# Expert tiles laid out in pairs: one weight load and 256-column operations for 14 of 23 tiles

## The chip, the cores and the metric

The kernel runs on one core of one Trainium2 chip. A core has TensorE (PE, and PEld for its weight loads), ScalarE (ACT), VectorE (DVE), GpSimd (POOL) and SyncE (SP), and 16 DMA engines that all queues share. The metric is the device time of one execution in microseconds, lower is better; the time given is the median of the runs.

## What is computed

The input is 16 sequences of 256 tokens with 128 features, 4096 tokens in all, in float32. Two layers follow each other. Each is a sandwich: half a mixture of experts, attention, half a mixture of experts, each on the layer-normalized input and added to it.

```python
x = x + 0.5 * ffn0(layernorm(x))     # 8 routed experts, top 2 by softmax, and a shared one; SwiGLU, 128 wide
x = x + attn0(layernorm(x))          # 16 heads of 8, difference of two softmaxes, a layer norm on the output
x = x + 0.5 * ffn0(layernorm(x))
x = x + 0.5 * ffn1(layernorm(x))     # 8 experts, top 2, shares normalized; a * gelu(g), 256 wide
x = x + attn1(layernorm(x))          # 16 heads of 8, causal, with an output projection
x = x + 0.5 * ffn1(layernorm(x))

# ffn1, for each token t and each of its two experts e:
hidden = xt[t] @ W1[e] + b1[e]
a, g = split(hidden)
out[t] += share[t, e] * ((a * gelu(g)) @ W2[e] + b2[e])
```

The reference computes every expert for every token and weights by zero where an expert isn't chosen. Only the two chosen experts count.

## The kernel before

**Parts and stages.** The 4096 tokens are 8 blocks of 512 (four chunks of 128). A part of an expert layer is two blocks, 1024 tokens and so 2048 pairs of token and expert. The first part of the first expert layer is computed densely, every expert for every token (`dense`), which fills the start. All other parts are sparse (`Sparse`): seven of two blocks in layer 0, seven of two blocks and two of one block in layer 1. The attention of a block runs in between, sequence by sequence (`Attention`).

**A sparse part.** `dispatch` normalizes the blocks, computes the gates, chooses two experts for each token (`choose`), and counts on VectorE how many tokens each expert has. Tiles of 128 slots belong to one expert each. With `nch` chunks there are `2 * nch + E - 1` tiles: 23 for two blocks, 15 for one, enough for any routing with 8 experts. `first` is the number of tiles of the earlier experts, `slot` the place of each token, `idx` its two slots. `scatter` writes the normalized rows to `slots_x` in HBM with indirect DMAs on GpSimd. Then `dispatch` compares the tile's number with each expert's `end` and so finds the expert of each tile; `rows` holds its row in `wcat`, an HBM array with all weights and biases of one expert side by side.

`load_tiles` works in steps of two tiles. For each tile SyncE reads a register from `rows` and issues one DMA of that expert's weights into a buffer of `b_wt` (257 KB in layer 0, 450 KB in layer 1); every second step it loads four tiles of `slots_x` into `xg`. `compute` takes two tiles: two transposes on TensorE, a copy into `xT`, then the first matmuls. For each tile, each half z of the hidden layer and each 128 hidden features k there is one matmul of 128 columns, with its own weights, into the PSUM buffer `hid` (tiles `big`). ScalarE applies bias and activation, in operations of 128 columns because the bias belongs to the tile's expert; layer 0 needs two of them for each (`swiglu`), layer 1 one. VectorE adds the other bias and multiplies into `h`. The second matmuls have `h` as the stationary operand and give tokens on partitions. VectorE adds the output bias tile by tile into `y`, SyncE writes `y` to `slots_y`. When all tiles of a part are stored, `combine` gathers each token's two rows on GpSimd and `add_to_x` adds them with their shares on VectorE.

**What sets the order.** Every engine's order is written out when the kernel is built. Each piece of work is a generator that says with `Ask` which engine it needs, what it reads and which buffers it takes. `Tasks.run` starts, again and again, the piece with the smallest expected start plus `HASTE` times its rank. `Clocks` and `Timed` keep the expected times; `MARGIN` is a slack by engine. The ranks of the parts (`FFN_RANK`) and of the attention of each block (`ATT_RANK`) are lists of numbers. Each engine then executes in the written order, and a later instruction does not pass one that waits.

**Buffers.** Three `big` PSUM buffers of two banks are shared by attention scores and hidden layers; two further banks are cut into halves (`half`). `b_wt` has six buffers and gets three more, and `b_xg` two and three more, from tiles of the dense stage (`rw`, `cwb` in the profile) once that is done. So a group `big<-xT,rw` does the same work as `big<-xT,wt`, and `cwb<-slots_x` is a load of `xg`. Nearly all operations are recorded at line 136, that of the helper that passes them on, so the profile's groups are told apart by their tiles.

A float32 matmul appears in the trace as two passes, each with a weight load.

Of the kernel before, what the change touches and what calls it, by code (L numbers as in the profile page):

```python
# [9 lines left out]
FP = mybir.dt.float32  # L10
BF = mybir.dt.bfloat16
I32 = mybir.dt.int32
# [13 lines left out]
TABLE = 2.0  # L26
LATE = 1.5
LATE_ROWS = 2.0
MARGIN = {"PE": 1.0, "ACT": 1.25, "DVE": 1.5, "POOL": 1.25, "SP": 2.0}
HASTE = 0.0048  # L30

FFN_RANK = [
    [63, 53, 104],
    [190, 217, 235, 249],
    [218, 230, 258, 292],
    [422, 440, 392, 493, 452],
]
ATT_RANK = [
    [75, 122, 109, 110, 131, 132, 238, 239],
    [259, 260, 308, 281, 348, 311, 320, 528],  # L40
]


# [210 lines left out]
def kernel(ctx: ExitStack, tc: tile.TileContext, a: dict, out: bass.AP):  # L254
# [37 lines left out]
    PCH = PB * NCH  # L292
    NTILE = 2 * PCH + E - 1
    NSLOT = NTILE * P
    BIG = 1 << 14
    assert NSLOT < BIG

# [41 lines left out]
    def buffers(n, shape, name, dtype=FP):  # L339
# [26 lines left out]
            for i in range(4)  # L366
# [23 lines left out]
                tile_of(shape, name)  # L390
                for name, shape in (
                    ("cntb", [P, P]), ("pos", [P, PCH * E + E]), ("low", [P, PCH, E]),
                    ("high", [P, PCH, E]), ("slot", [P, PCH, E]), ("over", [P, NTILE, E]),
                    ("little", [P, 128]),
                )
            )
# [156 lines left out]
        (a["L0_ffn_rw1"], a["L0_ffn_rw2"], a["L0_ffn_rb2"]),  # L553
        (a["L1_ffn_W1"], a["L1_ffn_W2"], a["L1_ffn_b2"]),
    ]
    wcat = [dram.tile([E * P, WC[layer]], FP, name=f"wcat{layer}") for layer in range(2)]

    for layer in range(2):
        clocks.expect(wcat[layer], E // 4 + KF[layer] + 2)

    def gather_weights(layer, b1t, *deps):
        w1, w2, b2 = srcs[layer]
        wc, col = wcat[layer], W1C[layer]
        v = wc.rearrange("(e p) f -> e p f", p=P)
        todo = [(v[e : e + 4, :, 0:col], w1[e : e + 4]) for e in range(0, E, 4)]
        for k in range(KF[layer]):
            todo += [(v[:, :, col : col + C], w2[:, k * P : (k + 1) * P, :])]
            col += C
        todo.append((v[:, :, col : col + C], b2.unsqueeze(1).to_broadcast([E, P, C])))
        col += C  # L570
        nk = 2 * KF[layer]
        for o, i in todo:
            yield Ask("SP", after=max(0.0, clocks.bytes_free - 3.0))
            nc.sync.dma_start(out=o, in_=i)
        yield Ask("SP", deps, after=max(0.0, clocks.bytes_free - 3.0))
        nc.sync.dma_start(
            out=wc[:, col : col + nk].rearrange("(e p) k -> p e k", p=P),
            in_=b1t.rearrange("p (e k) -> p e k", k=nk),
        )
# [34 lines left out]
    same = tile_of([P, E], "same")  # L614
    sums_ce = tile_of([P, PCH * E + E], "sums_ce")

    full = tile_of([P, E, PCH], "full")
    bare.gpsimd.iota(
        full, pattern=[[0, E], [P, PCH]], base=0, channel_multiplier=0,
        allow_small_or_imprecise_dtypes=True,  # L620
    )
    number = tile_of([P, NTILE, E], "number")
    bare.gpsimd.iota(
        number, pattern=[[1, NTILE], [0, E]], base=0, channel_multiplier=0,
        allow_small_or_imprecise_dtypes=True,
    )

    own4 = tile_of([P, 4, G], "own4")
    bare.gpsimd.memset(own4, 1.0)
# [325 lines left out]
    idx_of, rows_of, wgt_of = [], [], []  # L955
    for i in range(NFFN):
        idx_of.append(tile_of([P, 2, PCH], f"idx{i}", I32))
        rows_of.append(tile_of([P, NTILE], f"rows{i}", I32))
        wgt_of.append(tile_of([P, 2, PCH], f"wgt{i}"))

    def transfers(todo, when=None, pool=None):
# [16 lines left out]
    class Sparse:  # L978
        def __init__(self, index, layer, which, blocks, slots, rank, last=False):
            self.layer, self.last, self.rank = layer, last, rank  # L980
            self.after = 3 * layer + 2 * which
            self.blocks = blocks
            self.nch = len(blocks) * NCH
            self.ntile = 2 * self.nch + E - 1
            self.sx, self.sy = slots_x[slots], slots_y[slots]
            self.rows = rows_of[index]
            self.idx, self.wgt = (t[index][:, :, : self.nch] for t in (idx_of, wgt_of))
            self.gated = self.out_tiles = self.stored = 0
            self.scattered, self.weighed = [], False
            self.ready = False  # L990
            self.left = [NCH * 2 + (BPB if layer == 0 else 0) for _ in self.blocks]
# [20 lines left out]
        def dispatch(self):  # L1012
# [5 lines left out]
            for i, n in enumerate(self.blocks):  # L1018
# [9 lines left out]
            nch, ntiles = self.nch, self.ntile  # L1028
            cntb, pos, low, high, slot, over, little = tmp
            low, high, slot = (t[:, :nch] for t in (low, high, slot))  # L1030
            over = over[:, :ntiles]
            s3, N = [P, nch, E], nch * E

            tk = taken.rearrange("p c e -> p (c e)")
            cnt, ntile, first, end = (little[:, 16 * i : 16 * i + w] for i, w in enumerate((1, E, E, E)))
            _, (t,) = yield pe(taken, take=[(half, 1)])
            nc.tensor.matmul(t[:N, 0:1], lhsT=tk, rhs=ones[:, 0:1], start=True, stop=True)
            yield vec(t)
# [11 lines left out]
            nc.vector.tensor_tensor(  # L1050
                pv, pos[:, :E].unsqueeze(2).to_broadcast([P, E, nch]), full[:, :, :nch], ALU.is_gt
            )
            nc.vector.tensor_reduce(ntile, pv, AX.X, ALU.add)
            pe2 = over.rearrange("p n e -> p (n e)")[:, : E * E].rearrange("p (e f) -> p e f", e=E)
            nc.vector.tensor_tensor(
                pe2, earlier, ntile.unsqueeze(1).to_broadcast([P, E, E]), ALU.mult
            )
            nc.vector.tensor_reduce(first, pe2, AX.X, ALU.add)
            nc.vector.tensor_tensor(end, first, ntile, ALU.add)
            nc.vector.tensor_scalar(first, first, float(P), None, ALU.mult)  # L1060
            nc.vector.tensor_tensor(
                slot, pos[:, E : N + E].rearrange("p (c e) -> p c e", e=E),
                first.unsqueeze(1).to_broadcast(s3), ALU.add,
            )

            yield vec(slot)
            at = little[:, 64 : 64 + 2 * nch].rearrange("p (j c) -> p j c", j=2)
# [6 lines left out]
            tasks.add(self.rank - 6, self.scatter(xns))  # L1074

            yield vec(end)
            expert = cntb[:, :ntiles]
            nc.vector.tensor_tensor(
                over, number[:, :ntiles], end.unsqueeze(1).to_broadcast([P, ntiles, E]), ALU.is_ge
            )  # L1080
            nc.vector.tensor_reduce(expert, over, AX.X, ALU.add)
            nc.vector.tensor_scalar(self.rows[:, :ntiles], expert, float(E - 1), float(P), ALU.min, ALU.mult)
            self.ready = True

            yield vec(at, low)
# [85 lines left out]

        def load_tiles(self):

            layer, ntiles = self.layer, self.ntile
            for j in range(0, ntiles, 2):
                js = range(j, min(j + 2, ntiles))
                _, wts = yield Ask(
                    "SP", (self.rows, wcat[layer]), take=[(b_wt, len(js))],
                    when=lambda: self.ready and len(self.scattered) == 2 * self.nch,
                )  # L1180
                if j % 4 == 0:
                    n = min(4, ntiles - j)
                    _, at = bare.values_load_multi_w_load_instructions(
                        self.rows[0:1, j : j + n], engines=[ENG.SP], min_val=0, max_val=(E - 1) * P,
                        skip_runtime_bounds_check_because="a minimum of E - 1 and a count, by P",
                    )
                    clocks.free["SP"] += 0.8
                for i, wt in zip(js, wts):
                    row = at[i % 4]
                    clocks.free["SP"] += 0.2  # L1190
                    nc.sync.dma_start(out=wt[:, : WC[layer]], in_=wcat[layer][bass.ds(row, P), :])
                if j % 4 == 0:
                    _, (xg,) = yield Ask("SP", (self.sx,), take=[(b_xg, 1)])
                    ld = nc.sync.dma_start(
                        out=xg[:, :n],
                        in_=self.sx[j * P : (j + n) * P, :].rearrange("(i p) d -> p i d", p=P),
                    )
                    for s in self.scattered:
                        tc.add_manual_dep(ld.ins, s.ins.name, SYNC, reason="every row may be here")
# [2 lines left out]

        def compute(self, j, wts, xg, i0, last):
            layer = self.layer
            K, n = KF[layer], len(wts)
            w2, bias = W1C[layer], W1C[layer] + K * C + C
            act0, lin0 = (0, 1) if layer == 0 else (K, 0)
            _, (t, xT) = yield pe(xg, take=[(half, 1), (b_xT, 1)])
# [4 lines left out]
            yield from move(xT[:, : n * P], t[:, : n * P])  # L1213
            half.put(t)
            _, (hid, h) = yield pe(xT, *wts, take=[(big, 1), (b_h, 1)])
            at = [(i, k, slice((i * K + k) * P, (i * K + k + 1) * P)) for i in range(n) for k in range(K)]
            for z, base in ((0, act0), (1, lin0)):
                for i, k, cs in at:
                    nc.tensor.matmul(
                        hid[:, z, cs], lhsT=wts[i][:, (base + k) * P : (base + k + 1) * P],  # L1220
                        rhs=xT[:, i * P : (i + 1) * P], start=True, stop=True,
                    )
            b_xT.put(xT)
            tiles = [
# [1 line left out]
                    cs, wts[i][:, bias + act0 + k : bias + act0 + k + 1],  # L1226
                    wts[i][:, bias + lin0 + k : bias + lin0 + k + 1],
                )
                for i, k, cs in at
            ]  # L1230
            if layer == 0:
                yield from swiglu(hid, h, tiles)
# [16 lines left out]
                    start=(k == 0), stop=(k == K - 1),  # L1249
                )  # L1250
            b_h.put(h)
            for i in range(n):
                yield vec(t)
                nc.vector.tensor_tensor(
                    y[:, i, :], t[:, i * P : (i + 1) * P], wts[i][:, w2 + K * C : w2 + (K + 1) * C],
                    ALU.add,
                )
            half.put(t)
            b_wt.put(*wts)

            self.out_tiles += n
            late = 3.0 if self.out_tiles < self.ntile else 0.0
# [451 lines left out]
```

## Time and profile before

| | |
|---|---|
| Median of 3 timed runs | 1543.52 us (1541.05 to 1553.22) |
| The profiled execution | 1429.88 us, span 1428.2 us |
| Mean granted TensorE clock in the span | 0.93 |
| Bytes moved by DMA | 232.87 MB, mean 163 GB/s |
| Weight loads of expert tiles | 235 into `wt`, 117 into `rw` |
| Dispatches (indirect DMAs) | 240 scatters, 240 gathers |

The profiled execution is shorter than the timed runs by 113.6 us. All durations of instructions are from it, so sums are to be compared with its own time.

A row of a group gives the line, engine, operation, tiles written and read, shape and count; then the busy time in us and the mean duration of one in ns; then the idle time of the engine just before them and what ended it. The busy time of a group counts overlapping instructions once, so busy time divided by the count is what one costs in a dense run, and the mean is what one takes from its start to its end. A row by stretches gives for each engine the busy time and the number of instructions, then the granted TensorE clock, the mean busy share of the DMA engines and the rate.

### The profile page before, as it was taken

Reading aid. Unit: us, or ns where it says so; the run is one execution under the profiler, and the core shown is the slowest. Engines: PE = TensorE matmul, PEld = TensorE weight load, DVE = VectorE, ACT = ScalarE, POOL = GpSimd, SP = SyncE. Lnnn points to the kernel's source line nnn. Section 1 sums busy time; section 2 is a strip of 40 time slices with the busy share of each in tenths; the row PEclk is TensorE's granted clock in tenths of the full one; section 3 lists DMA queues with packets and bytes.
Section 4 is the critical chain, followed back from the end, with each engine's and each line's share of the span. In section 5 each row is a group of like instructions: output and inputs, shape, how many; then the busy total and the mean of one; then the engine's idle time right before and its main releaser. Section 6 shows DMA issues by size and latency. Waiting matters only on the chain. (4 is left out here: it accounts for less than half of the span.)

```text
span 1428.2 us, 29288 instructions
## 1 busy us (share of the span) xinstructions
PE 1189.7 (83%) x9730; PEld 810.9 (57%) x9730; DVE 932.9 (65%) x3259; ACT 803.2 (56%) x1710; POOL 612.9 (43%) x623
## 2 busy tenths in 40 slices
PE   5848899998989999998888888888679888887773
PEld 3414566555445544566755755676367676657672
DVE  5456876867555667674776778877854763885553
ACT  2212477766767776775666565556437665554331
POOL 2010545431630143616154466453752764665324
PEclk8766999999999999999999999999879999999997
DMA  5075577753125111567656655772168544658893
GB/s 121 20 165 150 184 201 207 196 166 93 53 89 140 40 27 35 177 198 229 194 160 215 203 155 170 231 230 88 45 226 254 170 169 156 206 191 283 271 305 111
DMA packets 207532, 232.87 MB, mean 163 GB/s; under 512 B 32062, under 2 KB 151545, under 8 KB 207371
## 3 DMA queue, kind: packets, MB, share of 16 engines
q1 hardware_dynamic: 192010, 199.42, 46.4%
q0 software_dynamic: 15360, 31.49, 7.0%
q8 instruction: 79, 1.29, 0.4%
q14 instruction: 83, 0.67, 0.2%
HBM read 183.84 MB, written 52.75 MB: 166 GB/s over the span
## 5 line engine op out<-in xcount | busy, mean ns | idle before, releaser
L136 ACT ACTIVATE ex<-big 128x1024 f32<-128x1024 f32 (+1 forms) x384 | 349.1, 957 | 76.8 <-PE big L136 71.4
L1117 POOL DMA_INDIRECT slots_x<-xn,idx x240 | 239.8, 999 | 213.8 <-PE bank L136 62.4
L1276 POOL DMA_INDIRECT g<-slots_y,idx x240 | 238.7, 994 | 196.2 <-PE big L136 75.1
L136 PE MATMUL big<-q,k 32*128 32x512 f32 (+1 forms) x1536 | 235.4, 613 | 5.5 <-DVE h L136 3.3
L136 PE MATMUL big<-xT,wt 128*128 128x128 f32 x1452 | 202.0, 285 | 15.6 <-ACT xT L136 9.9
L136 PEld LDWEIGHTS big<-xT,wt 128*128 128x128 f32 x1452 | 183.8, 199 | 29.1 <-ACT xT L136 16.0
L136 POOL TENSOR_TENSOR rstd<-rstd,mhalf 128x4 f32<-128x4 f32 (+1 forms) x64 | 62.1, 970 | 319.3 <-DVE rstd L136 311.6
L136 PE MATMUL bank<-ex,vaug 128*32 128x256 f32 (+1 forms) x3072 | 177.6, 371 | 11.7 <-DVE ex L136 4.1
L136 ACT ACTIVATE s<-big,wt 128x128 f32<-128x128 f32 x470 | 137.9, 384 | 69.1 <-PE big L136 56.9
L136 DVE SCALAR_TENSOR_TENSOR h<-big,wt,s 128x128 f32<-128x128 f32 x363 | 105.9, 342 | 47.5 <-ACT s L136 46.4
L136 PEld LDWEIGHTS bank<-ex,vaug 128*32 128x32 f32 x3072 | 89.8, 111 | 81.7 <-issue 13.6
L136 PE MATMUL bank<-wt,h 128*128 128x128 f32 x726 | 116.2, 294 | 21.4 <-DVE h L136 7.6
L136 DVE SCALAR_TENSOR_TENSOR x<-g,wgt,x 128x128 f32<-128x128 f32 x240 | 86.7, 364 | 71.8 <-DMA g<-slots_y,idx 70.6
L136 PEld LDWEIGHTS bank<-wt,h 128*128 128x128 f32 x726 | 96.9, 199 | 52.3 <-ACT xT L136 12.2
L136 ACT COPY xT<-bank 128x256 f32<-128x256 f32 x183 | 63.2, 375 | 110.6 <-PE bank L136 82.5
L136 PE MATMUL big<-xT,rw 128*128 128x128 f32 x720 | 107.4, 289 | 5.1 <-ACT xT L136 2.9
L136 PEld LDWEIGHTS big<-q,k 32*128 32x128 f32 x1536 | 74.9, 186 | 64.2 <-issue 39.4
L136 DVE TENSOR_TENSOR y<-bank,wt 128x128 f32<-128x128 f32 x235 | 59.2, 283 | 70.0 <-PE bank L136 34.4
L136 PEld LDWEIGHTS big<-xT,rw 128*128 128x128 f32 x720 | 96.5, 203 | 10.0 <-ACT xT L136 4.2
L136 POOL TENSOR_TENSOR ex<-ex,causal 128x512 f32<-128x512 f32 x52 | 65.5, 1281 | 77.8 <-ACT ex L136 68.2
L136 ACT COPY avs<-bank 128x256 f32<-128x256 f32 x96 | 36.1, 376 | 91.2 <-PE bank L136 68.0
L136 ACT ACTIVATE s<-big,rw 128x128 f32<-128x128 f32 x234 | 70.9, 382 | 17.7 <-PE big L136 16.8
(192 smaller groups left out, 1819.4 us busy)
## 6 DMA issues: line engine op xcount, KB each, us to landing
wt<-wcat SPq DMA_DIRECT2D x128, 450.0 KB
rw<-wcat SPq DMA_DIRECT2D x63, 450.0 KB
wt<-wcat SPq DMA_DIRECT2D x107, 257.0 KB
slots_y<-y SPq DMA_DIRECT2D x168, 128.0 KB
rw<-wcat SPq DMA_DIRECT2D x54, 257.0 KB
cwb<-slots_x SPq DMA_DIRECT2D x45, 256.0 KB
xg<-slots_x SPq DMA_DIRECT2D x31, 256.0 KB
slots_x<-zero SPq DMA_DIRECT2D x12, 384.0 KB
```

The source lines that it names most:

```text
L136: r = f(*args, **kw)
L1117: s = bare.gpsimd.indirect_dma_start(out=self.sx[:, :], out_offset=bass.IndirectOffsetOnAxis(ap=self.idx[:, j, c : c + 1], axis=0), in_=ro ...
L1276: s = bare.gpsimd.indirect_dma_start(out=g[:, :], out_offset=None, in_=self.sy[:, :], in_offset=bass.IndirectOffsetOnAxis(ap=self.idx[:, j ...
```

## The change

The slots of a part are laid out anew. Each expert's tiles are first taken in twos: `own[:, 0]` counts an expert's pairs of tiles, `own[:, 1]` its odd tile (0 or 1). All pairs come first in the slots, then the single tiles. The first `nch - 1` steps of two tiles are always pairs of one expert: 7 for a part of two blocks (14 of 23 tiles), 3 for a part of one block (6 of 15). The remaining 9 tiles are single ones, as before. The counts are such that this holds for any routing; an eighth pair, where there is one, lies in two single tiles.

A unit is a pair or a single tile; a part has 16 of them (12 with one block). `rows` holds one entry for each unit and `load_tiles` issues one weight load for each. In `compute`, a pair has one set of weights. Its first matmuls, its activations, its products and its bias addition are single operations on both tiles, 256 columns wide, where there were two of 128. For that `hid` and `h` are ordered by hidden feature first and tile second. Transposes, second matmuls, copies to `xT` and stores of `y` stay.

In `dispatch`, the counting is done for pairs and singles at once (twice as wide), the slot of a token gets a further term `beyond` where its place lies behind its expert's pairs, and the expert of a unit comes from two comparisons, one for the pairs and one for the singles, the latter counted from the end. `wcat` becomes twice as tall with the weights in the upper half, since the sum of the two comparisons starts at 8.

`HASTE`, two margins and the ranks have other numbers.

```diff
-MARGIN = {"PE": 1.0, "ACT": 1.25, "DVE": 1.5, "POOL": 1.25, "SP": 2.0}
-HASTE = 0.0048
+MARGIN = {"PE": 1.0, "ACT": 1.0, "DVE": 1.5, "POOL": 1.25, "SP": 1.5}
+HASTE = 0.003
 FFN_RANK = [
-    [63, 53, 104],
-    [190, 217, 235, 249],
-    [218, 230, 258, 292],
-    [422, 440, 392, 493, 452],
+    [80, 66, 114],
+    [190, 217, 315, 246],
+    [218, 225, 258, 290],
+    [424, 437, 433, 444, 408],
 ]
 ATT_RANK = [
-    [75, 122, 109, 110, 131, 132, 238, 239],
-    [259, 260, 308, 281, 348, 311, 320, 528],
+    [77, 132, 109, 110, 131, 132, 158, 159],
+    [319, 320, 342, 339, 406, 369, 373, 551],
 ]
...
+            self.npair = self.nch - 1
+            self.nunit = self.npair + E + 1
...
+            nc.vector.tensor_reduce(own[:, 0], pv[:, :, 1::2], AX.X, ALU.add)
             nc.vector.tensor_reduce(ntile, pv, AX.X, ALU.add)
-            pe2 = over.rearrange("p n e -> p (n e)")[:, : E * E].rearrange("p (e f) -> p e f", e=E)
+            nc.vector.scalar_tensor_tensor(own[:, 1], own[:, 0], -2.0, ntile, ALU.mult, ALU.add)
+            s4 = [P, 2, E, E]
...
             nc.vector.tensor_tensor(
-                pe2, earlier, ntile.unsqueeze(1).to_broadcast([P, E, E]), ALU.mult
+                pe2, earlier.unsqueeze(1).to_broadcast(s4), own.unsqueeze(2).to_broadcast(s4), ALU.mult
             )
             nc.vector.tensor_reduce(first, pe2, AX.X, ALU.add)
-            nc.vector.tensor_tensor(end, first, ntile, ALU.add)
-            nc.vector.tensor_scalar(first, first, float(P), None, ALU.mult)
-            nc.vector.tensor_tensor(
-                slot, pos[:, E : N + E].rearrange("p (c e) -> p c e", e=E),
-                first.unsqueeze(1).to_broadcast(s3), ALU.add,
-            )
+            nc.vector.tensor_tensor(end, first, own, ALU.add)
+            nc.vector.tensor_scalar(start, first[:, 0], 2.0 * P, None, ALU.mult)
+            nc.vector.tensor_scalar(inside, own[:, 0], 2.0 * P, None, ALU.mult)
+            nc.vector.scalar_tensor_tensor(beyond, end[:, 0], 2.0, first[:, 1], ALU.mult, ALU.add)
+            nc.vector.tensor_scalar(
+                beyond, beyond, -float(P), float(P * (ntiles - 1)), ALU.mult, ALU.add
+            )
+            place = pos[:, E : N + E].rearrange("p (c e) -> p c e", e=E)
+            yield vec(pos)
+            nc.vector.tensor_tensor(slot, place, start.unsqueeze(1).to_broadcast(s3), ALU.add)
+            nc.vector.tensor_tensor(low, place, inside.unsqueeze(1).to_broadcast(s3), ALU.is_ge)
+            nc.vector.tensor_tensor(low, low, beyond.unsqueeze(1).to_broadcast(s3), ALU.mult)
+            nc.vector.tensor_tensor(slot, slot, low, ALU.add)
...
+            nc.vector.tensor_scalar(start, end[:, 0], 2.0, -2.0 * self.npair, ALU.mult, ALU.add)
             nc.vector.tensor_tensor(
-                over, number[:, :ntiles], end.unsqueeze(1).to_broadcast([P, ntiles, E]), ALU.is_ge
+                over[:, :, 0:E], number[:, -self.nunit :], start.unsqueeze(1).to_broadcast(s3u), ALU.is_ge
+            )
+            nc.vector.tensor_tensor(
+                over[:, :, E:], follow[:, -self.nunit :], end[:, 1].unsqueeze(1).to_broadcast(s3u), ALU.is_ge
             )
...
             for j in range(0, ntiles, 2):
-                js = range(j, min(j + 2, ntiles))
+                nwt = 1 if u < self.npair else min(2, ntiles - j)
                 _, wts = yield Ask(
-                    "SP", (self.rows, wcat[layer]), take=[(b_wt, len(js))],
+                    "SP", (self.rows, wcat[layer]), take=[(b_wt, nwt)],
...
-            K, n = KF[layer], len(wts)
+            K, n = KF[layer], min(2, self.ntile - j)
+            one = len(wts) < n
+            wts = wts * n if one else wts
...
-            at = [(i, k, slice((i * K + k) * P, (i * K + k + 1) * P)) for i in range(n) for k in range(K)]
+            at = [(i, k, slice((k * n + i) * P, (k * n + i + 1) * P)) for i in range(n) for k in range(K)]
+            if one:
+                both = [(0, k, slice(k * n * P, (k + 1) * n * P)) for k in range(K)]
+            else:
+                both = at
             for z, base in ((0, act0), (1, lin0)):
-                for i, k, cs in at:
+                for i, k, cs in both:
                     nc.tensor.matmul(
                         hid[:, z, cs], lhsT=wts[i][:, (base + k) * P : (base + k + 1) * P],
-                        rhs=xT[:, i * P : (i + 1) * P], start=True, stop=True,
+                        rhs=xT[:, : n * P] if one else xT[:, i * P : (i + 1) * P], start=True, stop=True,
                     )
...
-            for i in range(n):
+            tn = t[:, : n * P].rearrange("p (i c) -> p i c", c=C)
+            for i in range(1 if one else n):
+                si = slice(0, n) if one else slice(i, i + 1)
+                b2 = wts[i][:, w2 + K * C : w2 + (K + 1) * C].unsqueeze(1)
                 yield vec(t)
                 nc.vector.tensor_tensor(
-                    y[:, i, :], t[:, i * P : (i + 1) * P], wts[i][:, w2 + K * C : w2 + (K + 1) * C],
-                    ALU.add,
+                    y[:, si, :], tn[:, si, :], b2.to_broadcast([P, si.stop - si.start, C]), ALU.add
                 )
```

## The prediction

> **What bounds the kernel now.** I read the page's head first, then the busy time by stages, then the groups with shapes kept apart, the waits of TensorE, and the transfers of the last stage. The page's chain of waits covers only the last 46 us, so the bound has to be read from the stages.
>
> ```profile
> span 1428.2 us, 29288 instructions
> PE 1189.7 (83%) x9730; PEld 810.9 (57%) x9730; DVE 932.9 (65%) x3259; ACT 803.2 (56%) x1710; POOL 612.9 (43%) x623
> ```
>
> ```profile
> core 0: us, PE busy (x) PEld busy (x) DVE busy (x) ACT busy (x) POOL busy (x), PEclk, DMA share, GB/s
> 0.00:160.00 160.00, 108.05 (x306) 58.11 (x307) 90.30 (x270) 39.21 (x78) 24.32 (x44) 0.77 0.50 127
> 160.00:640.00 480.00, 450.05 (x4034) 259.54 (x4032) 322.52 (x1128) 343.17 (x665) 177.36 (x183) 1.00 0.43 124
> 640.00:1000.00 360.00, 300.85 (x2520) 227.43 (x2523) 263.57 (x931) 214.46 (x479) 182.24 (x181) 0.94 0.61 188
> 1000.00:1080.00 80.00, 59.20 (x496) 42.28 (x489) 52.29 (x193) 35.83 (x78) 51.06 (x49) 0.83 0.42 143
> 1080.00:1280.00 200.00, 174.33 (x1601) 133.88 (x1599) 130.26 (x446) 124.31 (x267) 115.11 (x103) 0.96 0.59 187
> 1280.00:1405.00 125.00, 97.21 (x785) 89.65 (x785) 68.54 (x280) 46.23 (x146) 50.90 (x53) 0.95 0.85 277
> ```
>
> See here: from 160 to 640 us (mostly layer 0) TensorE is busy 450 of 480 us at full clock. It sets the pace, and only shorter TensorE work can help much. From 640 to 1405 us (mostly layer 1's experts) it is busy 631.6 of 765 us: 133 us are idle, the clock is below 1, and no other engine is full. That is a chain of hand-overs between engines, with the DMA engines at 0.85 in the last 125 us.
>
> ```profile
> L136 PE MATMUL big<-xT,wt 128*128 128x128 f32 x1452 | 202.0, 285 | 15.6 <-ACT xT L136 9.9 <-ACT ex L136 4.7 <-ACT s L136 0.4
> L136 ACT ACTIVATE s<-big,wt 128x128 f32<-128x128 f32 x470 | 137.9, 384 | 69.1 <-PE big L136 56.9 <-issue 8.5 <-ACT ex L136 1.0
> L136 DVE SCALAR_TENSOR_TENSOR h<-big,wt,s 128x128 f32<-128x128 f32 x363 | 105.9, 342 | 47.5 <-ACT s L136 46.4 <-PE bank L136 0.8
> L136 DVE TENSOR_TENSOR y<-bank,wt 128x128 f32<-128x128 f32 x235 | 59.2, 283 | 70.0 <-PE bank L136 34.4 <-ACT xT L136 13.4 <-ACT s L136 7.3
> L136 ACT ACTIVATE s<-big,b_0t 128x512 f32<-128x512 f32 x64 | 40.5, 684 | 59.1 <-PE big L136 56.7 <-issue 1.5 <-DVE h L136 0.7
> L136 DVE SCALAR_TENSOR_TENSOR h<-big,b_0t,s 128x512 f32<-128x512 f32 x32 | 23.9, 747 | 31.9 <-ACT s L136 31.9
> ```
>
> ```profile
> PE bank L136 <- DVE y L136: 20.0, 18, 3.8
> PE bank L136 <- ACT xnT L136: 16.0, 28, 2.0
> PE bank L136 <- DVE h L136: 15.9, 19, 2.0
> PE big L136 <- ACT xT L136: 12.8, 19, 2.0
> ```
>
> The first row is the experts' first matmul, the next three what follows it; the two with 512 columns give the price of width. In the waits, rows ending in y, h and xT belong to the expert chain that the change touches.
>
> **What the Trainium skill says.** "TensorE: Matmul & The Clock Gate", LDWEIGHTS: loading weights takes their columns divided by 1.2 GHz, 107 ns for 128, and it overlaps a running matmul. The trace agrees that a load costs little beside a matmul:
>
> ```profile
> 709.51 0.97 PEld L136 LDWEIGHTS big<-xT,wt 128*128 128x128 f32 x8
> 48.17 1.88 PE L136 MATMUL big<-xnT,rw 128*128 128x512 f32 x4
> ```
>
> Eight loads take 0.97 us, so (0.97 - 0.19) / 7 = 111 ns apart, the last one's 0.19 us (median) taken off. Four passes of 512 columns take 1.88 us, (1.88 - 0.59) / 3 = 429 ns apart, 0.84 ns a column. So a 128-column pass streams for about 107 ns and is paced at 111 ns with its load. "ScalarE: Activation LUTs", What ACT_TABLE_LOAD costs: an ACTIVATE with a pointer bias takes about 280 ns and 0.833 ns a column, and back to back they overlap by 93 ns. The trace has 384 ns for 128 columns (the formula gives 387), and 137.9 / 470 = 293 ns as they run together.
>
> **The change, part by part.** Seven parts of layer 0 and seven of layer 1 have 23 tiles, two of layer 1 have 15. So 7 x 7 = 49 pairs in layer 0 and 7 x 7 + 2 x 3 = 55 in layer 1 become one unit each: 104.
>
> *TensorE.* The instruction order shows 636 first matmuls of 128 columns replaced by 318 of 256; each is two passes in the trace (1452 rows for 726). A pair of passes costs 2 x 111 = 222 ns now; one of 256 columns 256 x 0.84 + 3 = about 218 ns. 636 x 4 ns = 3 us saved. Half the weight loads go, but they were covered by the streaming. Second matmuls and transposes stay.
>
> *ScalarE.* 416 activations of 128 columns become 208 of 256. Slope from the rows: (684 - 384) / 384 = 0.78 ns a column, so 293 + 100 = 393 ns. 416 x 0.293 - 208 x 0.393 = 122 - 82 = 40 us less busy time.
>
> *VectorE.* 318 products become 159: running 105.9 / 363 = 292 ns each, slope (747 - 342) / 384 = 1.05 ns, so 427 ns: 93 - 68 = 25 us less. 208 additions into y become 104: 59.2 / 235 = 252 ns against 252 + 134 = 386 ns: 12 us less. Against this each of 16 dispatches has ten more instructions: five on 8 columns (211 ns), a reduction (220), the place test (300), a product and an addition on 64 columns (223, 261), and a second comparison where one of 184 columns becomes two of 128 (0.2 us net), with wider neighbours 0.2: about 2.5 us, 40 us in all. VectorE ends level.
>
> *Chain of a pair.* Layer 1, activation to second matmul: 384 + 3 x 293 + 342 = 1605 ns now; 484 + 393 + 477 = 1354 ns after. The addition that frees the PSUM half: 283 + 252 = 535 against 417. Some 0.37 us less, 104 times: 38 us of chain. Most lies beside other work. The TensorE waits of this chain are 20.0 + 15.9 + 12.8 and 8.2 more for xT on the bank, 57 us; I let a quarter go, 14 us, since ScalarE's queue is also shorter. Ends: 0 (another producer is late next: xnT and the exponentials) and 30.
>
> *Loads.* 352 become 248; 49 x 257 KB + 55 x 450 KB = 37 MB of 233 go. Before the last stage the DMA share is 0.4 to 0.6, and I count nothing. In the last stage:
>
> ```profile
> DMA packets 24713, 34.67 MB, mean 277 GB/s; under 512 B 2336, under 2 KB 17369, under 8 KB 24697
> wt<-wcat SPq DMA_DIRECT2D x31, 450.0 KB
> rw<-wcat SPq DMA_DIRECT2D x18, 450.0 KB
> ```
>
> 49 loads would be 49 x 16 / 23 = 34; 15 x 0.45 MB at 277 GB/s is 24 us of transfer. TensorE idles 125 - 97.2 = 27.8 us there; I take 8 us. Ends: 0 (each wait is named after y, h or xT, not after a weight) and 20.
>
> *Clock.* The half-speed stretches behind the 0.83 to 0.96 stand after idle gaps; fewer gaps, 4 us. Ends 0 and 10.
>
> *Dispatch.* Its 2.5 us stand in VectorE's order in front of the products and additions of other parts, and 1.8 of them before the scatter on GpSimd, the weight loads on SP and then the tiles. From 160 to 640 us other parts cover it. At the start and near 1000 to 1080 us little is ready: I take 4 us. Ends: 0 and 40.
>
> *Ranks and margins.* They reorder every queue. By kind of matmul the order keeps its shape: three of 24 equal slices hold nearly no expert tiles, before and after, and the tail is the same (last half-part, store, eight gathers, addition). I take 0, ends 15 either way.
>
> Sum against the profiled execution (1429.88 us, span 1428.2): -3 - 14 - 8 - 4 + 4 = -25, so 1405 us, a ratio of 0.9825. The timed runs stand 7.9% above it (1543.52 against 1429.88), and no view shows where, so I scale: 1516.
>
> **The rivals.** *Larger gain:* TensorE's idle time in layer 1 falls by the upper ends: -3 - 30 - 20 - 10 + 4 = -59, ratio 0.959, 1480. For it: 133 us idle and a DMA share of 0.85. Against: the waits are spread over many small rows. *No difference:* the streamed columns are unchanged, ScalarE at 56% was never the bound, every wait freed is taken by the next; -3 + 4 and the loads hidden, 1543. For it: 450 of 480 us. Against: layer 1. *Slower:* the dispatch arithmetic is exposed. All 40 us on the path, with only the 3 of streaming and 12 of chain and loads regained: +25, ratio 1.0175, 1570. Its place is VectorE, whose written order delays y and h behind a dispatch. It decides once more than about 2 us of each dispatch's 2.5 become idle time on TensorE. For it: VectorE is at 65 to 73% in layers' middle, and y and h lead the waits. Against: 37 us leave the same queue. That fewer than 14 tiles are pairs is excluded: the loop makes seven pair units whatever the routing.
>
> **How the numbers follow.** Forecast 0.49 (own range 1490 to 1528), larger gain 0.17, no difference 0.17, slower 0.17. A change of about 1% is what this measurement can tell. Faster 0.66, same 0.17, slower 0.17. The range 1468 to 1566 covers the upper-end gain with some ordering luck, and most of the slower case.
>
> **What would show it.** Right: first-matmul busy time nearly equal, ScalarE near 763 us, VectorE within 15 us of 933, DMA 196 MB, TensorE's idle time from 640 us on down by some 25 us. Wrong: 160 to 640 us shrinking much (then ScalarE was the bound there), or idle time growing around the dispatches, or the gain all in stages that only the ranks moved.

## The result, and the profile after

The kernel after takes 1536.11 us (median of 12 runs, 1522.72 to 1546.06), the kernel before 1545.6 us beside it. The ratio is 0.9926, 95% interval 0.9897 to 0.9955. The forecast was 1516 us and 0.9825: the sign held, but only 11 of the 27 us that this ratio means here came, and 1536 lies outside the likeliest case's own range of 1490 to 1528.

Chips differ, and one reading of the profile depends on it. The first timings (their chip is not on record) and the first eight experiments (all on one chip) ran where the kernel before takes 1533 to 1546 us. The last eight ran on two other chips, four on each, and on both it takes 1434 us. I call these the first and the second kind. The profile of before that the prediction read (1429.88 us) fits the second kind, but its chip is not on record either. Ratios are always to the kernel before, timed beside; on the second kind the change was measured once on each chip, 0.9894 both times (intervals 0.9861 to 0.9927 and 0.9875 to 0.9913; 1420 us against 1434). Where it isn't said otherwise I compare traces of the second kind. The head of the page of the kernel after in its first profile, and then on the second kind:

```profile
span 1529.9 us, 27110 instructions
PE 1241.3 (81%) x9094; PEld 810.8 (53%) x9094; DVE 936.1 (61%) x3157; ACT 770.2 (50%) x1504; POOL 604.6 (40%) x620
```

```profile
span 1412.8 us, 27110 instructions
PE 1194.0 (85%) x9094; PEld 783.8 (55%) x9094; DVE 935.6 (66%) x3157; ACT 769.3 (54%) x1504; POOL 606.4 (43%) x620
```

VectorE, ScalarE and GpSimd are as busy on both; only TensorE and the span differ. The stretches on the second kind, in the columns shown for before:

```profile
160.00:640.00 480.00, 447.70 (x3798) 251.39 (x3796) 310.54 (x1077) 322.64 (x583) 170.38 (x174) 0.98 0.33 96
640.00:1000.00 360.00, 304.85 (x2327) 219.88 (x2327) 268.95 (x933) 200.91 (x409) 190.56 (x190) 0.93 0.52 159
1000.00:1080.00 80.00, 64.97 (x518) 45.94 (x517) 57.58 (x190) 37.69 (x76) 46.09 (x46) 0.91 0.44 139
1080.00:1280.00 200.00, 178.10 (x1516) 130.85 (x1516) 144.34 (x443) 123.74 (x245) 118.83 (x108) 0.97 0.52 163
1280.00:1390.00 110.00, 85.53 (x618) 77.03 (x616) 61.11 (x233) 41.29 (x113) 51.79 (x55) 0.91 0.74 224
```

From 160 to 640 us TensorE idles as before (32 of 480 us, 30 before). From 640 to 1390 us it is busy 633.5 of 750 us, so 117 us idle where 133 were. The operations of the pairs, groups with shapes apart:

```profile
L136 PE MATMUL big<-xT,wt 128*128 128x256 f32 x420 | 109.9, 403 | 5.9 <-ACT xT L136 4.1 <-ACT ex L136 1.5
L136 PE MATMUL big<-xT,wt 128*128 128x128 f32 x612 | 86.8, 286 | 1.5 <-ACT xT L136 1.5
L136 ACT ACTIVATE s<-big,wt 128x256 f32<-128x256 f32 x140 | 58.2, 478 | 33.4 <-PE big L136 19.8 <-issue 9.1 <-DVE st L136 2.6
L136 DVE SCALAR_TENSOR_TENSOR h<-big,wt,s 128x256 f32<-128x256 f32 x105 | 46.9, 477 | 23.4 <-ACT s L136 20.5 <-PE big L136 2.1 <-PE bank L136 0.6
L136 DVE TENSOR_TENSOR y<-bank,wt 128x256 f32<-128x256 f32 x70 | 29.0, 418 | 21.8 <-PE bank L136 13.4 <-ACT avs L136 4.4 <-ACT xT L136 1.7
```

The mean durations are the forecast ones (activation 484, product 477, addition 417 ns). TensorE's waits, the rows that answer to those shown of before:

```profile
PE bank L136 <- DVE y L136: 35.5, 25, 6.1
PE bank L136 <- DVE h L136: 15.0, 9, 8.3
PE bank L136 <- ACT xnT L136: 14.7, 23, 2.6
...
PE big L136 <- ACT xT L136: 10.1, 15, 2.5
```

Here is the surprise: the waits for ScalarE shrink, but that for `y`, an operation which itself became shorter, grows from 20.0 to 35.5 us. `y` stands in VectorE's order behind the dispatches, but the order itself is new too; the experiments split this growth.

### The profile page after: what moved, and what is told of

Its sections match the earlier page's. It is cut to its first block, busy times and chain, and to the rows that moved or that the text cites. A ratio compares the mean times of both kernels' runs of the same rounds, so it can differ in the third digit from the quotient of the medians.

```text
span 1529.9 us, 27110 instructions
## 1 busy us (share of the span) xinstructions
PE 1241.3 (81%) x9094; PEld 810.8 (53%) x9094; DVE 936.1 (61%) x3157; ACT 770.2 (50%) x1504; POOL 604.6 (40%) x620
## 5 line engine op out<-in xcount | busy, mean ns | idle before, releaser
L1156 POOL DMA_INDIRECT slots_x<-xn,idx x240 | 239.7, 999 | 363.9 <-PE bank L136 97.1
L136 PE MATMUL big<-q,k 32*128 32x512 f32 (+1 forms) x1536 | 257.5, 648 | 15.5 <-issue 7.3
L136 PE MATMUL big<-xT,wt 128*128 128x128 f32 (+1 forms) x1032 | 204.2, 343 | 17.1 <-ACT xT L136 7.0
L136 PEld LDWEIGHTS big<-xT,wt 128*128 128x128 f32 x1032 | 165.6, 210 | 38.5 <-issue 12.9
L136 ACT ACTIVATE s<-big,wt 128x128 f32<-128x128 f32 (+1 forms) x334 | 115.7, 417 | 101.8 <-PE big L136 39.9
L136 DVE SCALAR_TENSOR_TENSOR h<-big,wt,s 128x256 f32<-128x256 f32 (+1 forms) x258 | 92.2, 398 | 53.0 <-ACT s L136 48.3
L136 ACT COPY xT<-bank 128x256 f32<-128x256 f32 (+1 forms) x183 | 61.7, 374 | 105.3 <-PE bank L136 48.3
L136 PE MATMUL big<-xT,rw 128*128 128x128 f32 (+1 forms) x504 | 102.4, 342 | 10.7 <-issue 5.7
L136 DVE COPY oall<-bank 128x144 f32<-128x144 f32 x96 | 29.2, 304 | 133.4 <-PE bank L136 89.6
L136 PEld LDWEIGHTS big<-xT,rw 128*128 128x128 f32 x504 | 81.4, 206 | 22.1 <-issue 9.3
L136 DVE TENSOR_TENSOR y<-bank,wt 128x128 f32<-128x128 f32 (+1 forms) x167 | 54.1, 341 | 61.0 <-PE bank L136 38.1
```

The lines of the kernel that those rows point to most:

```text
L136: r = f(*args, **kw)
L1156: s = bare.gpsimd.indirect_dma_start(out=self.sx[:, :], out_offset=bass.IndirectOffsetOnAxis(ap=self.idx[:, j, c : c + 1], axis=0), in_=ro ...
```

## Experiments

"Order kept" below means that the planner was told the changed kernel's operations, while others were written out, so every queue keeps the changed kernel's order. The diffs are shortened and leave out the lines that tell the planner so.

**The order alone: lists and layouts crossed.** One kernel has the new layout with the old `FFN_RANK`, `ATT_RANK`, `MARGIN` and `HASTE`, the other the old layout with the new ones.

```diff
-HASTE = 0.003      # and the three tables: layout_only, from the kernel after
+HASTE = 0.0048
-HASTE = 0.0048     # and the three tables: ranks_only, from the kernel before
+HASTE = 0.003
```

> The changed kernel with the ranks, margins and haste of before: the layout alone. Theory A (the layout's gain is real and the new ranks add nothing): ratio to before 0.985 to 0.995, like the whole change. Rival B (the layout gains nothing and the ranks made the 0.7%): 1.00, within 0.4%. Rival C (the layout needs its own ranks; with the old ones its tiles come at the wrong time): 1.00 to 1.02. ScalarE's busy time near 770 us and DMA near 194 MB under all three.

> The kernel before with the ranks, margins and haste of the changed one. Theory A: 1.00, within 0.5%, since the ranks only reorder. Rival B: 0.99 to 0.995. Rival C: 1.00 to 1.02, the new ranks fit the new layout only. Work per engine as before in all three (ScalarE near 803 us, 232.9 MB by DMA).

Measured: 1598.33 us, ratio 1.0415 (1.0368 to 1.0462), and 1568.87 us, ratio 1.0228 (1.0183 to 1.0274). Either list on the other layout costs far more than the whole change gains, and both ratios lie above every range that was expected. (The planner also chooses the engine of some copies, so a new list moves a few of them: ScalarE has 1490 instructions in the first of the two, 1504 in the kernel after.) In the new layout with old lists, the late stretches read:

```profile
1280.00:1400.00 120.00, 91.09 (x769) 56.39 (x769) 72.70 (x216) 53.05 (x103) 65.44 (x57) 0.78 0.14 41
1400.00:1600.00 200.00, 135.48 (x910) 120.74 (x910) 99.97 (x389) 59.35 (x167) 81.65 (x85) 0.86 0.68 213
```

A repeat of the kernel before on that chip has:

```profile
1280.00:1400.00 120.00, 94.62 (x769) 71.62 (x765) 77.08 (x260) 59.00 (x129) 61.81 (x56) 0.84 0.45 145
1400.00:1600.00 200.00, 91.25 (x673) 85.95 (x673) 66.42 (x262) 39.86 (x131) 54.36 (x57) 0.89 0.51 161
```

The DMA share falls from 0.45 to 0.14 in the first stretch and rises to 0.68 in the last: expert tiles are left for the end, with hardly any attention beside them (32 of the 910 matmuls from 1400 us on apply its weights to the values).

**The same kernels again.** One profiled run of each on the first kind of chip.

> The kernel before unchanged, profiled once more, because its first profile (1429.9 us) is 7.5% under its timed runs (1545.6 us) while the profile of the changed kernel (1532.0 us) is like its timed runs. Theory D (the first profile left out stretches in which every queue stands still, and the timed runs have them): this profile spans 1535 to 1550 us, with TensorE idle time ended by nothing that the profile shows (5 us in the first profile, 51 us in that of the changed kernel). Rival E (the changed kernel brings these stretches itself): 1425 to 1435 us, none of them.

> The changed kernel unchanged, profiled once more. Theory D: 1525 to 1545 us with standstills at other places than in its first profile, or, if this execution has none of them as the first profile of before, about 1400 to 1420 us. Rival E: 1525 to 1545 us with the standstills at the same instructions.

Measured: 1543.14 us (span 1541.4) and 1524.33 us (span 1522.2). So the first profile of before, 113 us shorter, was no property of the kernel. TensorE's idle time that is ended by nothing the profile shows (5 us in that profile, 51 in the first one of the kernel after) is 44 and 31 us here, so the change doesn't bring it.

**The parts of the pairs, one at a time,** each from the kernel after, order kept:

```diff
 # split_ops: activations, products and additions of a pair in two halves
+for cs in halves(cs) if one else (cs,):
     nc.scalar.activation(s[:, cs], hid[:, 0, cs], AF.Gelu, bias=b)
 # split_mm: first matmuls of a pair as two of 128 columns
-rhs=xT[:, : n * P]
+rhs=xT[:, part * P : (part + 1) * P]      # for part in (0, 1)
 # two_loads: a second copy of each pair's weights, into HBM
+nc.sync.dma_start(out=dump[len(dumped) % len(dump)][:, : WC[layer]], in_=wcat[layer][bass.ds(at[u % 4], P), :])
```

> The changed kernel, every engine's order kept, but each pair's activations, products and bias addition issued as two operations of 128 columns again (416 more narrow ScalarE operations for 208 wide, 318 for 159 and 208 for 104 on VectorE). Theory A (merged operations carry the gain, as my sum had it: 40 us of ScalarE, 37 us of VectorE and the shorter chain): at least +0.9% over the changed kernel, ratio to before 1.001 to 1.015. Rival B (they lie beside the path, and the written order with its standstills sets the time): within 0.4% of the changed kernel, ratio 0.989 to 0.997.

> The changed kernel, every engine's order kept, but each pair's first matmul issued as two of 128 columns with the same weights loaded twice (636 for 318). Theory A (streaming is paced by columns, 4 ns a pass): +3 us, 0.2%, ratio to before 0.992 to 0.998. Rival B (fewer weight loads and fewer instructions on TensorE's queue are worth more than the streaming says): +1% or more, ratio above 1.00.

> The changed kernel, with each pair's weights moved a second time, by a DMA on the same queue behind the first one, into HBM where nobody reads it (104 more transfers of 257 or 450 KB, 37 MB in all). Theory A (loads count in the last stage alone): +5 to +10 us, ratio 0.995 to 1.002. Rival B (transfers are hidden everywhere): within 0.3% of the changed kernel, ratio 0.990 to 0.996. Rival C (the queue of SyncE and the DMA engines bound the tile stages): +1.5% or more, ratio above 1.007.

Measured against before: 1.0036 (1.0013 to 1.0060), 0.9971 (0.9944 to 0.9997), 0.9987 (0.9965 to 1.0008). Less the 0.9926 of the kernel after, the merged operations are worth 1.1% or 17 us, the 256-column matmuls 0.45% or 7 us, the saved loads 0.6% or 9 us, each uncertain by some 6 us. The kernel after was not timed beside these three (its one profiled run on that chip took 1524.33 us), so all three lean on the 0.9926 of the first timings, and their sum of 33 us is uncertain by some 15. It is still more than the change brought: something in it costs. Nobody waits for the second copies, and they take no buffer in SBUF, so the 9 us are the price of issuing and moving them alone.

**The dispatch arithmetic, more and less.** One kernel adds ten short VectorE instructions to each dispatch (results not used). The other keeps pairs and order but has the old nine instead of nineteen; it leaves out that both tiles of a pair belong to one expert.

```diff
 # dispatch_plus, dispatch_plus2
+for _ in range(2):
+    nc.vector.tensor_tensor(high, place, inside.unsqueeze(1).to_broadcast(s3), ALU.is_ge)
+    nc.vector.tensor_tensor(high, high, beyond.unsqueeze(1).to_broadcast(s3), ALU.mult)
+for _ in range(6):
+    nc.vector.tensor_tensor(little[:, 120:128], beyond, start, ALU.add)
 # dispatch_old, dispatch_old2: own, start, inside, beyond, low and the second comparison go
-nc.vector.tensor_tensor(low, place, inside.unsqueeze(1).to_broadcast(s3), ALU.is_ge)
...
+nc.vector.tensor_tensor(slot, place, first_o.unsqueeze(1).to_broadcast(s3), ALU.add)
```

> The changed kernel with the ten added VectorE instructions of each dispatch issued a second time, in front of the computation of the slots (two place tests and two products on 64 columns, six operations on 8 columns, about 2.2 us each, 16 times, 36 us of VectorE). Theory A (4 us of 40 on the path): +0.3%, ratio to before 0.993 to 0.999. Rival B (the dispatch arithmetic is exposed and ate the gain): +1.3% or more, ratio above 1.005.

> The changed kernel with pairs, merged operations and order of every queue kept, but with the nine short VectorE instructions of the kernel before in each dispatch instead of nineteen. It leaves out what the ten did: tokens are put behind each other as before, so a pair unit no longer holds one expert's tokens alone. Theory of the prediction (2.5 us of a dispatch mostly lie beside other work, 4 us of 40 exposed): about 4 us less than the changed kernel, ratio to before about 0.990. Rival (the arithmetic is exposed on VectorE, as doubling it suggested with 30 us for 36 us added): 20 to 30 us less than the changed kernel, ratio to before 0.973 to 0.980. If the tenfold extra in the doubled version hurt only because the planner knew nothing of it, taking the ten away brings less than half of that.

> The same kernel as dispatch_old (tokens not put behind each other in pairs), once more, to narrow its difference to the changed kernel beside the doubled arithmetic. It was 12 to 15 us faster than the changed kernel. Theory of the prediction: 4 us. Rival (mostly exposed): 20 to 30 us. If it is again near 14 us, 40% of the ten instructions' 36 us are exposed, and both were off.

> The same kernel as dispatch_plus, ten more VectorE instructions in each dispatch, beside the one with ten fewer. If the exposed share is one and the same on both sides, it is as much slower than the changed kernel as dispatch_old2 is faster. If the share grows with the length of the arithmetic (each further instruction has less other work to lie beside), it is 25 to 32 us slower, as it was on its first chip, and dispatch_old2 12 to 15 us faster.

Measured on the first kind of chip: dispatch_plus 1.0125 (1.0063 to 1.0188), so 2.0% or 30 us above the kernel after, uncertain by 10. On the second kind: dispatch_old 0.9807 (0.9774 to 0.9841) and 0.9826 (0.9805 to 0.9846), dispatch_plus2 1.0081 (1.0064 to 1.0099), with the kernel after at 0.9894 each time. So ten fewer give 12.5 and 9.8 us, about 11, and ten more cost 27 us, each uncertain by about 4 us. VectorE's busy time and the wait for `y` with ten fewer (second run):

```profile
PE 1197.4 (85%) x9094; PEld 784.1 (56%) x9094; DVE 909.8 (65%) x2997; ACT 769.1 (55%) x1504; POOL 608.1 (43%) x620
```

```profile
PE bank L136 <- DVE y L136: 29.1, 25, 6.1
```

Ten more:

```profile
PE 1212.4 (84%) x9094; PEld 793.9 (55%) x9094; DVE 965.0 (67%) x3317; ACT 769.7 (53%) x1504; POOL 606.9 (42%) x620
```

```profile
PE bank L136 <- DVE y L136: 43.5, 30, 8.1
```

One group shows what a short instruction costs in the kernel after:

```profile
L136 DVE TENSOR_SCALAR little<-little 128x8 f32<-128x8 f32 x64 | 9.3, 172 | 0.6
```

The ten are worth 935.6 - 909.8 = 25.8 us of VectorE time, 1.6 us a dispatch; 11 of them, 43%, show in the span. The next ten are 29.4 us, and 27, or 92%, show. So the first ten were covered by more than half, the next ten hardly. Why is not shown. The dispatch may have become too long for the work beside it; but the ten more also stand in one block in front of the scatter and were unknown to the planner, while of the ten that go eight stood in front of the scatter and the order had been made with all nineteen.

The waits of TensorE for `y` go 29.1, 35.5, 43.5, those for `h` 11.1, 15.0, 19.0. Laying the traces of the kernel after and of dispatch_plus2 side by side (same matmuls, same order), the latter is 1 us late at 144 us, 12 at 242, 17 at 640, 18 at 724, 28 at 1000, still 28 at 1120 and 37 at the end. These two executions are the fastest and the slowest of their kernels, whose medians lie 27 us apart, so only the shape counts: a third comes with the first three of the sixteen dispatches (they stand at 146, 180 and 236 us), and nothing near 1000 to 1080 us.

**Contents against order.** All of it taken back at once, order kept: halves, 128-column matmuls, second copies of weights, nine instructions. It leaves out the same as dispatch_old, and nobody waits for its second copies.

```diff
 # all_undone = split_ops + split_mm + two_loads + dispatch_old
```

> The changed kernel's order of every queue, but with the operations of the kernel before: the merged ScalarE and VectorE operations in two halves, the first matmuls as two of 128 columns, a second copy of each pair's weights, and the nine short VectorE instructions per dispatch instead of nineteen (so tokens are not put behind each other in pairs, and the second copies go to HBM and not to SBUF). What is left against the kernel before is the order alone. Theory of the prediction (operations and loads are worth 25 us, the order nothing): 1.0175 times the changed kernel and 1.00 of the kernel before. Rival (the merges are worth some 33 us and the arithmetic costs 12 to 30 us, so 3 to 21 us net; the order makes up the rest): 1.002 to 1.014 times the changed kernel, so 0.993 to 1.005 of the kernel before.

> The changed kernel as it is, as the base for the three beside it. Expected between the two ratios measured so far, 0.9894 and 0.9926 of the kernel before.

Measured: 1431.63 us, 0.9985 (0.9967 to 1.0003). So the new order with the old operations is worth about 2 us, at most some 5; with a second tile waiting for its own weights, as in the kernel before, it could be worth less, and the pairs so much more. From there to dispatch_old (0.9807 and 0.9826, mean 0.9817) the pairs are worth 0.0168 or 24 us, uncertain by 4; and the arithmetic takes 11 back. The waits for `y` in this kernel (L1382 is the addition of a pair in halves):

```profile
PE bank L136 <- DVE y L136: 21.0, 12, 6.0
PE bank L136 <- DVE y L1382: 15.7, 13, 3.9
```

That is 36.7 us with the old operations and the old dispatch. So the growth of this row from 20.0 us came with the new order, though the time stayed the same; the pairs bring it down to 29.1, and the arithmetic raises it to 35.5. A row of waits alone doesn't tell what a change costs.

Summing the gaps in which neither a matmul nor a load ran, by the engine that ended them, in traces of the second kind and in the first one of before:

| kernel | TensorE idle | ended by ScalarE | by VectorE | TensorE busy | clock |
|---|---|---|---|---|---|
| before | 208.1 | 97.1 | 100.2 | 1189.7 | 0.930 |
| all undone | 197.7 | 87.0 | 100.9 | 1205.2 | 0.925 |
| after | 191.0 | 78.4 | 106.8 | 1194.0 | 0.929 |
| ten fewer (second run) | 184.1 | 79.8 | 98.5 | 1197.4 | 0.928 |
| ten more | 210.2 | 78.6 | 126.5 | 1212.4 | 0.914 |

Repeats of a kernel differ by up to 6 us in busy time. The dispatch moves the VectorE column alone. From before to after ScalarE's column falls by 19 and VectorE's rises by 7; within one order, from all undone to after, it is -9 and +6.

**The order's own scatter.** The kernel after with one number of the planner changed by 3%, and the two controls of the kernel as it is:

```diff
-HASTE = 0.003
+HASTE = 0.0031
```

> The changed kernel with the planner's weight on ranks at 0.0031 instead of 0.003 and nothing else: every instruction is the same, their order differs in many places. It measures how much time an order written without any tuning of its own costs. Theory of the prediction (ranks and margins are worth nothing, ends 15 us either way): within 15 us of the changed kernel, ratio to before 0.983 to 1.002. Rival (each layout needs a list of its own, and the order is worth as much as the layout): 10 to 60 us slower than the changed kernel, since 0.003 was the one its lists were made for; ratio 1.00 to 1.03.

> The changed kernel as it is, measured beside the three that follow, so that they have a base on the same chip. Expected 0.9926 of the kernel before, as measured first (0.9897 to 0.9955); nothing else hangs on it. If it comes out outside 0.989 to 0.996, the small ratios of the earlier experiments need wider margins than their intervals.

Measured: 1442.43 us, 1.0066 (1.0046 to 1.0086), so 1.7% or 24 us above the kernel after, by the order and a few copies that changed their engine with it (ScalarE 1501 instructions for 1504).

**A shorter dispatch.** The whole computation, with three instructions fewer in each dispatch, order kept:

```diff
-nc.vector.tensor_reduce(own[:, 0], pv[:, :, 1::2], AX.X, ALU.add)
-nc.vector.tensor_reduce(ntile, pv, AX.X, ALU.add)
+nc.vector.tensor_reduce(own, pv.rearrange("p e (k a) -> p a e k", a=2), AX.X, ALU.add)
...
+    pe2, scaled, own.unsqueeze(2).to_broadcast(s4), ALU.mult     # scaled: earlier * (P, 2 * P)
```

> The changed kernel, whole, with its dispatch arithmetic rewritten: the two counts by one reduction over odd and even tiles, the table of earlier experts scaled by the tile sizes beforehand, the scaling of the unit numbers moved into their tables, so sixteen short VectorE instructions in a dispatch instead of nineteen; order of every queue kept. Three instructions of about 0.21 us less in 16 dispatches are 10 us. Theory of the prediction: 1 us less than the changed kernel, not visible. Rival (exposed): about 8 us less, 0.5%, ratio to before about 0.987, which would be the fastest of these kernels.

Measured: 1418.39 us, 0.9884 (0.9850 to 0.9918) beside 0.9894: not told apart. VectorE's busy time fell by 4.5 us (935.6 to 931.1), not 10, since the instructions that stayed do more; by the 43% above that would be 2 us, below what this comparison can see. I have no version that is certainly faster than the kernel after.

## Why the prediction was right and where it was wrong

**The bound was read rightly.** From 640 us on TensorE's idle time fell from 133 to 117 us, by some 17 of the 25 forecast. Stretches of fixed length can't show whether layer 0 became shorter, but all_undone and dispatch_old2 have the same order of matmuls: of the 22 us between their traces the pairs had gained 4 by 640 us. ScalarE's busy time fell to 769 us (763 forecast), VectorE's stayed level (935.6), the bytes fell to 194.5 MB (196).

**The pairs' own terms nearly held.** Streaming, pair chain, loads and clock were put at 3 + 14 + 8 + 4 = 29 us; together they measured 24, uncertain by 4. For streaming, the busy time of all first matmuls (the instructions that touch `xT`; no column for GpSimd), before and after:

```profile
0.00:1450.00 1450.00, 287.86 (x2172) 269.56 (x2172) 0.29 (x1) 63.15 (x183) 0.93 0.53 161
0.00:1450.00 1450.00, 284.72 (x1536) 233.11 (x1536) 0.42 (x1) 61.72 (x183) 0.93 0.45 134
```

TensorE's column falls by 3 us, as forecast, which is no more than repeats differ (287.5 in another execution of the kernel after); splitting them alone cost 7, uncertain by 6. The rows by weight buffer must not be added here: matmuls on `wt` and on `rw` overlap, and the sums would be 309.4 and 295.6. Chain and loads measured 17 and 9 where 14 and 8 were taken. The clock term stays open. The two traces have 0.930 and 0.929, but the executions timed on the second kind have a mean granted clock of 0.923 and 0.922 before (21 and 27 runs) and 0.926 and 0.927 after (6 and 5). Were all of TensorE's 1190 us to follow, that would be an estimated 4 to 5 us, but no run separates it from the shorter time itself.

**The step that failed is the dispatch.** It said: 40 us of arithmetic, "I take 4 us", cover from 160 to 640 us and little at the start and near 1000 us. Its amount was too large (25.8 us; the eight-column instructions, for one, have a mean of 172 ns and 9.3 / 64 = 145 ns of busy time where 211 was taken), but its exposed part too small: 11 us, 43%. Taking 7 us more here leaves 18 of the 25. The cover from 160 to 640 us was wrong as well: in the trace with ten more, 11 of the lag's 37 us arise there, and none where layer 1 was expected to be thin, near 1000 to 1080. The rival "slower" had the mechanism right: with more arithmetic TensorE waits longer for `y` and `h`. It decides beyond 2 us of idle time a dispatch; the trace has 11 / 16 = 0.7.

**Ranks: the value held, the ends didn't.** The new order is worth about 2 us where 0 was taken. But the ends of 15 us are what lists fitted to a layout deserve, not what an order deserves: the same layout with a list of another was 4.9% slower (1.0415 against 0.9926), and a 3% change of one weight cost 24 us. The forecast of 25 us was as large as the scatter of the quantity it set to zero; that it came near zero is owed to lists made for this layout.

In sum: -24 for the pairs, +11 for the dispatch, -2 for the order, which is -15 us of 1434. That it meets the measured 0.9894 is no test, since each step was measured against the next. Against the 25 forecast, 7 us are missing by the dispatch and 5 by the pairs, the latter hardly beyond their uncertainty; the order gives 2 back. In the first timings the change brought 11 us; its interval overlaps with the other two. The scaling by 7.9% changed no ratio. The gap it bridged fits a difference between chips, so no view of the kernel could show it.

## What to carry to other kernels

Arithmetic put in front of other work on an engine that executes in a written order is not free because the engine is 65% busy: ask which waits stand behind it (here those for `y` and `h`), and don't carry the covered share of the first microseconds over to the next ones. When a change comes with new priorities, build the old operations in the new order: one such kernel separates what the operations give from what the order gives, and keeps you from reading a row of waits that the order moved as the work of the change. Before explaining a gain of 1%, change the order a little and see what that alone does.

## What was not expected of the hardware

- The kernel before takes 1533 to 1546 us on the first kind of chip and 1434 us on the second. In the two traces of the kernel after, with nearly the same order of instructions, VectorE and ScalarE are as busy on both (936 and 770 us); TensorE has 1241 and 1194 us at a granted clock of 0.898 and 0.929, and its idle time is 261 and 191 us. Of these 70 us more, 48 are ended by nothing that the profile shows (51 us against 3). The lag arises in small steps from about 160 us to the end. What causes them is open; no run here separates it.
- More idle time came with slower matmuls. Ten more instructions a dispatch raised TensorE's idle time by 19 us and, in these two executions, its busy time by 18 us for the same matmuls (by 13 against another execution of the kernel after). The first of the traces has 26 stretches at half the clock, the second 32, and the clock was 0.923 to 0.930 in the eleven timed executions of the one on the second kind and 0.914 to 0.919 in the six of the other.
- Merging two 128-column operations saved less on VectorE than on ScalarE, but not by much. Over both weight buffers, and overlaps counted once, an activation of 256 columns has 415 ns of busy time against 2 x 280, a saving of 145 ns; a product has 445 ns against 2 x 287, a saving of 129 ns. From the Trainium skill ("ScalarE: Activation LUTs", What ACT_TABLE_LOAD costs) one activation of 256 columns with a pointer bias comes to an estimated 280 + 256 x 0.833 = 493 ns; the trace has 478.
